# A convolution and whitening kernel: three image groups last instead of two, three x tiles instead of four, and homes for three quarters of the last output piece

## The chip, the core and the metric

The kernel runs on one core of a Trainium2 chip. The metric is the device time of one execution in microseconds (us), and lower is better. The engines are named as the profile names them: PE (matrix products), PEld (its weight loads), DVE (vector), ACT (scalar), POOL and SP. SP issues most DMAs here. A DMA issued by SP or ACT goes through a hardware queue, one issued by POOL through a software queue. All of them move their bytes through the same 16 DMA engines.

## The reference, cut to what matters

Two layers on `x` of shape (4, 64, 256, 256), float32. The first is a long convolution in two dimensions, separable per channel, with filters made by a small sine network. The second whitens the 64 channels: it forms a covariance from every ninth pixel of all four images, takes its inverse square root by five Newton-Schulz steps, and multiplies every pixel by it.

```python
k = jnp.einsum('ijk,imk->ijmk', hx, hy)[0]        # one 256x256 filter per channel
y = jnp.fft.irfft2(u_f * k_f, s=(fft_size, fft_size))[..., :L, :L]
out = y + x * bias[:, None, None]                 # layer 0
...
x1_s = x1[:, ::STRIDE ** 2]
cov = x1_s @ x1_s.T / x1_s.shape[1] + EPS * jnp.eye(B, dtype=x.dtype)
deconv = _isqrt_newton_schulz(cov, N_ITER)
out = deconv @ (x1 - mean1)                       # layer 1
```

No pixel of the output can be made before all four images have gone through layer 0, because the inverse square root needs them all. In what follows "the root" is the short chain from the covariance to the whitening matrix `W`.

## The kernel before, in words

**Convolution.** The 64 channels are cut into 8 groups `g` of 8 channels. A step is one (g, image n) pair, 32 steps in all, and one `x` tile (128 partitions x 4096 float32, 2 MB) holds a step. Inside a step the loop goes over `c` = 0, 2, 4, 6, two channels at a time. I number these quarters of steps by `k = 4 * i + c // 2`, from 0 to 127, and call each one a turn. In turn `k`, `group` (line 394) multiplies the two new channels by the first Toeplitz factor and the two channels of two turns ago by the second one. DVE then adds the bias term in place in the `x` tile (line 412), and `store` (line 420) writes the two finished channels to the DRAM scratch `y_d` with two DMAs of 256 KB.

**Order of the steps.** `steps` (line 107) runs groups 0 to 5 over all images first, and then, image by image, groups 6 and 7. Image 0 is thus complete after step 25, image 1 after 27, image 2 after 29, image 3 after 31. `covariance(n - 1)` (line 572) runs when group 7 of the next image begins, at c = 2, that is in front of the products of turns 109, 117 and 125, and once more after the loop. `blocks` (line 370) says in which turn each of the eight parts of a Toeplitz tile is loaded; three such tiles exist.

**Loads of x.** There are four `x` tiles. In turn (i, c) SP issues the load of the same quarter of step i + 2 (line 588).

**Pieces.** The output is made in 32 pieces of 2 MB (`pieces`, line 344): eight per image, each 128 partitions x 4096. Before the root, pieces can be loaded back from `y_d` into buffers that have become free. There are 13 such homes (line 347): two extra buffers `e`, four sample buffers `s`, three Toeplitz buffers `t`, four x tiles `i`. The table `early` (line 378) gives the turns after which the first nine loads are issued: 106, 108, 110, 112, 117, 120, 124, 125, 126. The other four follow after the last covariance input (line 613). The first piece of image 0 needs `y_d[0]` complete.

**After the root.** For each piece (line 619) PE makes four windows of 1024 columns, ACT and DVE add the shift in place (lines 639 and 640), and the result is stored. Piece 0 goes out in four 512 KB parts, pieces 1, 30 and 31 in two 1 MB parts, all others in one 2 MB store. Stores of pieces 1 to 18 are issued by POOL, the others by SP. After piece i is stored, SP waits for that store and loads piece i + 13 into its home (line 647).

**Queues.** The convolution and the root are written out by hand in each engine's order (`tc.manual_schedule`, line 557). SP carries out its DMAs in that order; a wait at the head of its queue holds back all that follows. Each hardware-queue DMA also takes one of eight semaphores in turn and waits for the DMA that had it before, so at most eight of them are on their way at once.

Of the kernel before, what the change touches and what calls it, by code (L numbers as in the profile page):

```python
# [38 lines left out]
F32 = mybir.dt.float32  # L39
I32 = mybir.dt.int32  # L40
AF = mybir.ActivationFunctionType
ALU = mybir.AluOpType
# [3 lines left out]
NB, C, L = 4, 64, 256  # L46
P, H2 = 128, 2
EMB, ORDER = 33, 64
PIX = L * L
CG = 8  # L50
HP = P // 2
STEP = 9
# [2 lines left out]
EPS = 0.01  # L55
N_ITER = 5
GW = P + L
FP = 4096

TURN = 6.283185  # L60
# [4 lines left out]
def conv_whiten_kernel(ctx: ExitStack, tc: tile.TileContext, a: dict, out: bass.AP):  # L65
# [1 line left out]
    x = a["x"]  # L67

    const = ctx.enter_context(tc.tile_pool(name="const", bufs=1))
    xpool = ctx.enter_context(tc.tile_pool(name="xpool", bufs=4))  # L70
    epool = ctx.enter_context(tc.tile_pool(name="epool", bufs=2))
    spool = ctx.enter_context(tc.tile_pool(name="spool", bufs=NB))
    tpool = ctx.enter_context(tc.tile_pool(name="tpool", bufs=3))
    o1pool = ctx.enter_context(tc.tile_pool(name="o1pool", bufs=4))
# [25 lines left out]
    def load_x(t, g, n, c):  # L100
        nc.sync.dma_start(
            out=t[:, c : c + 2],
            in_=x[n, g][:, c : c + 2],
        )


    steps = [(g, n) for g in range(C // CG - 2) for n in range(NB)]
    steps += [(g, n) for n in range(NB) for g in range(C // CG - 2, C // CG)]

    x_tiles = [xpool.tile([P, CG, H2, L], F32, tag="in", name=f"x{u}") for u in range(4)]  # L110
    for c in range(0, CG, 2):
        load_x(x_tiles[0], *steps[0], c)
        if c == 0:
            nc.sync.dma_start(out=decay, in_=a["decay"])
    nc.sync.dma_start(out=mask, in_=a["mask"])
# [1 line left out]

    ident = const.tile([P, P], F32, tag="ident", name="ident")
    make_identity(nc, ident)
    samp = []  # L120
    for n in range(NB):
        t = spool.tile([P, FP], F32, tag="samp", name=f"samp{n}")
        samp.append(
            t[:, 0 : H2 * NJ * (C + 1)].rearrange("p (b j c) -> p b j c", b=H2, j=NJ)
        )
        nc.gpsimd.memset(samp[n][:, :, :, C : C + 1], 1.0)
        nc.gpsimd.memset(samp[n][:, :, NJ - 1, 0:C], 0.0)
# [199 lines left out]
    def covariance(n):  # L327
# [17 lines left out]


    homes = [
        {"t": (tpool, "toep"), "s": (spool, "samp"), "i": (xpool, "in"), "e": (epool, "extra")}[k]
        for k in "eetssiistitis"
    ]  # L350

    def load_y(i):

        n, q = pieces[i]
        pool, tag = homes[i % len(homes)]
        t = pool.tile([P, FP], F32, tag=tag, name=f"yi_{n}_{q}")
        nc.sync.dma_start(out=t, in_=y_d[n][:, q * FP : (q + 1) * FP])  # L357
        return t

    def load_next():  # L360
        loaded[len(loaded)] = load_y(len(loaded))

    loaded = {}
    todo = []
    pending = []

# [2 lines left out]


    blocks = {}
    for g in range(1, C // CG):
        first = 16 * g - 14 if g < C // CG - 1 else 16 * g - 22
        for part in range(8):
            k = first + (part * 12 // 8 if g < C // CG - 2 else part)
            blocks[k // 4, k % 4 * 2] = (g, part)

    early = {
        (26, 4): 1, (27, 0): 1, (27, 4): 1, (28, 0): 1, (29, 2): 1, (30, 0): 1, (31, 0): 1, (31, 2): 1, (31, 4): 1
    }  # L380
    orders = [list(range(L // HP)), list(reversed(range(L // HP)))]

    credit = [0.0]
# [35 lines left out]

    def store(second):  # L420
        g, n, c, yt, _ = second
        halves = g >= C // CG - 2
        for b in range(H2):
            row = b * C + g * CG + c
            nc.sync.dma_start(
                out=y_d[n][row : row + 2, :].rearrange("c (p w) -> p c w", w=L),
                in_=yt[:, c : c + 2, b],
            )

        if c == CG - 2 and (g, n) != steps[-1]:  # L430
            todo.extend(pack_ops(g, n, yt, slice(CG // 2 if halves else 0, CG)))
        elif c == CG // 2 - 2 and halves:
            todo.extend(pack_ops(g, n, yt, slice(0, CG // 2)))
# [13 lines left out]
    def place(width, rows=P):  # L447
        if not room or room[-1][1] + width > H2 * L:
            t = o1pool.tile([P, H2 * L], F32, tag="o1", name=f"chain{len(room)}")
            room.append([t, 0])  # L450
        t, at = room[-1]
        room[-1][1] += width
        return t[0:rows, at : at + width]
# [6 lines left out]
    def whitening(i15, ones):  # L460
# [86 lines left out]
        Z = Zs[(N_ITER - 2) % 2]  # L547
        pw = product(T, Z, "pw")
        spin(2)
        W = place(C)  # L550
        nc.vector.tensor_scalar(W, pw[:, 0:C], rs, None, ALU.mult)
        shift = const.tile([P, 1], F32, tag="shift", name="shift")
        nc.scalar.activation(shift, pw[:, C : C + 1], AF.Copy, scale=nrs)
# [3 lines left out]
    with tc.manual_schedule(  # L557
        engines={engines.PE, engines.SP, engines.DVE, engines.Activation, engines.Pool}
    ):
        toep = {0: new_toeplitz(0)}  # L560

        for f, lo, hi in ((0, 0, 2), (0, 2, 4), (0, 4, 6), (1, 0, 2), (0, 6, 8), (1, 2, 4), (1, 4, 8)):
            for half in range(2):
                load_toeplitz(toep[0], 0, f, half, lo, hi, nc.scalar if half else nc.sync)
        for c in range(0, CG, 2):
            load_x(x_tiles[1], *steps[1], c)
        for i, (g, n) in enumerate(steps):
            xt = x_tiles[i % 4]
            for c in range(0, CG, 2):
                item = (g, n, c, xt, [])  # L570
                if g == C // CG - 1 and n > 0 and c == 2:
                    covariance(n - 1)
                if len(pending) == 2:
                    group(item, pending.pop(0))
                else:
                    half_group(item, 0)
                pending.append(item)
                if i == 0 and c == 6:

                    fold = const.tile([P, C], F32, tag="fold", name="fold")  # L580
                    nc.vector.tensor_tensor(fold, ident[:, 0:C], ident[:, C:P], ALU.add)

                    nc.scalar.activation(bf[:, 0:1], samp[0][:, 0, 0, C : C + 1], AF.Sqrt)
                if i == 1 and c < CG - 2:
                    load_pick(c // 2 * 3, c // 2 * 3 + 3)

                if i + 2 < len(steps):
                    load_x(x_tiles[(i + 2) % 4], *steps[i + 2], c)
                if (i, c) in blocks:
                    tg, part = blocks[i, c]  # L590
                    if part == 0:
                        toep[tg] = new_toeplitz(tg)
                    lo = part % 2 * CG // 2
                    load_toeplitz(toep[tg], tg, part // 4, part // 2 % 2, lo, lo + CG // 2)
                for _ in range(early.get((i, c), 0)):
                    load_next()
        g, n, c, yt, _ = pending[0]
        for item in pending:
            half_group(item, 1)
            pack(1.0)  # L600
            store(item)

        pack()
        i15 = place(2 * C, rows=C).rearrange("p (u c) -> p u c", u=2)
        for u in range(2):
            nc.gpsimd.tensor_scalar(i15[:, u], ident[0:C, 0:C], 1.5, None, ALU.mult)  # L606
        ones = place(P, rows=C)
        nc.gpsimd.memset(ones, 1.0)
        for lo in range(CG // 2, CG, 2):
            pack_by_pe(g, n, yt, slice(lo, lo + 2))  # L610
        spin(4)
        covariance(NB - 1)
        while len(loaded) < len(homes):
            load_next()
        W, shift = whitening(i15, ones)


    halves = [slice(u * C, (u + 1) * C) for u in range(2)]
    for i, (n, q) in enumerate(pieces):
        yt = loaded.pop(i)  # L620

        v = yt.rearrange("p (v f) -> p v f", v=2)
        o = out[n, q].rearrange("p (v f) -> p v f", v=2)

        part = 512 if i == 0 else 1024 if i == 1 or i > len(pieces) - 3 else 2048
        for w in range(FP // 1024):


            cols = slice(w * 512, (w + 1) * 512)
            po = [  # L630
                psA.tile([P, 512], F32, tag="psA", name=f"po_{n}_{q}_{w}_{u}") for u in range(2)
            ]
            for k in range(2):
                for u in range(2):
                    nc.tensor.matmul(  # L635
                        po[u][halves[k]], lhsT=W[halves[u]], rhs=v[halves[u], k, cols],
                        start=True, stop=True,
                    )
            nc.scalar.activation(v[:, 0, cols], po[0], AF.Identity, bias=shift)  # L639
            nc.vector.tensor_scalar(v[:, 1, cols], po[1], shift, None, ALU.add)  # L640
            end = (w + 1) * 512
            if end % part == 0:

                issue = nc.sync if i == 0 or i + len(homes) >= len(pieces) else nc.gpsimd
                issue.dma_start(out=o[:, :, end - part : end], in_=v[:, :, end - part : end])  # L645
        if i + len(homes) < len(pieces):
            loaded[i + len(homes)] = load_y(i + len(homes))


def _constants():  # L650
# [55 lines left out]
```

## Time and profile before

| what | value |
|---|---|
| median of 3 runs | 902.47 us (902.0 to 902.86) |
| span of the profiled execution | 902.1 us |
| PE busy | 781.2 us, 87% of the span |
| DVE busy | 581.5 us, 64% |
| ACT busy | 395.5 us, 44% |
| moved by DMA | 285.61 MB, 317 GB/s over the span |
| line 220, convolution products, share of the chain that ended last | 64% |
| last convolution product ends | 613.6 us |
| first whitening product begins | 643.25 us |

The profiled execution lasted 902.1 us by its span, which lies inside the range of the three runs and 0.37 us under their median. The profile shows no time around that span. Up to 613.6 us the chain that ended last is almost all PE. From there to 643.25 us it is the packing of the last samples, the last covariance and the root. After that PE is on the chain only for short stretches, and the rest is DMA.

### The profile page before, as it was taken

The numbers are of one execution on the slowest core, as the hardware profiler recorded it, in microseconds if no ns is written. First come the engines' busy times: TensorE is split into PE (matmuls) and PEld (weight loads), VectorE is DVE, ScalarE is ACT, GpSimd is POOL, SyncE is SP. The second block draws the span as 40 slices with busy tenths as digits, with TensorE's granted clock in tenths as the row PEclk, the third lists the DMA queues.
The fourth block names the chain that finished last, engine by engine and source line by source line (L and its number), as shares of the span: only waits on it lengthen the run. The fifth ranks groups of instructions, "written<-read, shape, count | busy, mean of one in ns | idle before, by whom it ended". The sixth has DMA issues, their size and how long they took to land.

```text
span 902.1 us, 28046 instructions
## 1 busy us (share of the span) xinstructions
PE 781.2 (87%) x11928; PEld 647.5 (72%) x11928; DVE 581.5 (64%) x801; ACT 395.5 (44%) x676; POOL 14.5 (2%) x40
## 2 busy tenths in 40 slices
PE   8999999999999999999999999999999565666200
PEld 7999999999999999999999999999533111212000
DVE  3487778877888778877888877877688332233200
ACT  2655554545455555545454444442487232233200
POOL 1000000000000000000000000000010000000000
PEclk9999999999999999999999999999999766866755
DMA  7988889798788888888997899979999999999998
GB/s 209 327 262 252 242 261 271 234 273 251 247 263 261 244 264 259 258 250 267 293 275 241 285 351 356 335 237 390 375 401 429 430 432 432 429 434 430 430 430 355
DMA packets 117912, 285.61 MB, mean 317 GB/s; under 512 B 8891, under 2 KB 91116, under 8 KB 110108
## 3 DMA queue, kind: packets, MB, share of 16 engines
q1 hardware_dynamic: 113436, 244.94, 79.0%
q0 software_dynamic: 3056, 37.95, 10.0%
q8 instruction: 95, 1.56, 0.7%
q10 hardware_dynamic: 1296, 0.93, 0.4%
q14 instruction: 29, 0.24, 0.1%
HBM read 149.35 MB, written 134.44 MB: 315 GB/s over the span
## 4 chain that ended last, share of the span: by engine, by line
PE 74%; DMA 11%; another core or an unknown queue 7%; DVE 0%; issue 0%; SPq 0%; ACT 0%; POOLq 0%; DVEq 0%
PE p L220 64%; DMA out_dram<-yi 5%; DMA yi<-y_d 5%; PE po L635 4%; PE pc L333 2%; PE ph L252 1%; PE pk L300 1%; PE spin L442 1%; DMA toep<-g_d 0%; PE busy L152 0%; PE pm L158 0%; SPq L357 0%; DMA scratch<-in_zw_dram 0%; DVE yi L640 0%
## 5 line engine op out<-in xcount | busy, mean ns | idle before, releaser
L220 PE MATMUL p<-toep,x 64*64 64x64 f32 (+3 forms) x5040 | 579.5, 284 | 0.8 <-issue 0.8
L220 PE MATMUL p<-toep,o 64*64 64x64 f32 (+3 forms) x5040 | 579.5, 284 | 0.0
L220 PEld LDWEIGHTS p<-toep,x 64*128 64x128 f32 (+1 forms) x5040 | 535.7, 166 | 24.4 <-issue 1.3
L220 PEld LDWEIGHTS p<-toep,o 64*128 64x128 f32 (+1 forms) x5040 | 536.7, 166 | 10.7 <-issue 0.2
L409 ACT COPY o<-p 64x512 f32<-64x512 f32 x504 | 292.8, 581 | 294.2 <-PE p L220 286.6
L319 DVE COPY_PREDICATED samp<-mask,x 128x464 f32<-128x464 int32 (+3 forms) x351 | 297.2, 847 | 9.8 <-DVE x L412 0.2
L412 DVE SCALAR_TENSOR_TENSOR x<-x,bias,p 128x512 f32<-128x512 f32 x252 | 179.8, 744 | 121.3 <-PE p L220 117.3
L635 PE MATMUL po<-yi,chain 64*64 64x512 f32 x1024 | 143.7, 720 | 60.4 <-DMA yi<-y_d 60.4
L640 DVE TENSOR_SCALAR yi<-po,shift 128x512 f32<-128x512 f32 x128 | 96.1, 751 | 109.0 <-PE po L635 100.7
L635 PEld LDWEIGHTS po<-yi,chain 64*64 64x64 f32 x1024 | 48.0, 162 | 155.2 <-issue 150.5
L639 ACT ACTIVATE yi<-po,shift 128x512 f32<-128x512 f32 x128 | 88.0, 687 | 116.7 <-PE po L635 116.0
L333 PE MATMUL pc<-samp 128*64 128x65 f32 x464 | 14.9, 223 | 0.0
L333 PEld LDWEIGHTS pc<-samp 128*64 128x64 f32 x464 | 14.3, 137 | 0.3
L645 POOL DMA_DIRECT2D out_dram<-yi x19 | 10.5, 554 | 130.5 <-DMA out_dram<-yi 55.1
L606 POOL TENSOR_SCALAR chain<-ident 64x64 f32<-64x64 f32 x2 | 1.0, 519 | 606.6 <-PE ph L252 606.6
L286 DVE COPY o<-ph 64x256 f32<-64x256 f32 x8 | 3.4, 422 | 9.7 <-PE ph L252 9.6
L152 PE MATMUL busy<-idle 128*128 128x128 f32 x64 | 9.4, 307 | 0.0
L152 PEld LDWEIGHTS busy<-idle 128*128 128x128 f32 x64 | 8.9, 222 | 0.2 <-issue 0.2
L300 PE MATMUL pk<-x,pick 128*128 128x56 f32 (+1 forms) x72 | 8.3, 292 | 0.0
L300 PEld LDWEIGHTS pk<-x,pick 128*128 128x128 f32 x72 | 8.1, 192 | 0.1
L442 PE MATMUL spin<-ident 128*128 128x128 f32 x50 | 7.9, 292 | 0.0
L286 ACT COPY o<-ph 64x256 f32<-64x256 f32 x8 | 2.9, 368 | 10.7 <-DMA toep<-g_d 9.2
(93 smaller groups left out, 77.4 us busy)
## 6 DMA issues: line engine op xcount, KB each, us to landing
x<-in_x_dram SPq DMA_DIRECT2D x128, 512.0 KB, 5.3
y_d<-x SPq DMA_DIRECT2D x256, 256.0 KB, 3.5
yi<-y_d SPq DMA_DIRECT2D x32, 2048.0 KB, 15.6
out_dram<-yi POOLq DMA_DIRECT2D x17, 2048.0 KB, 67.7
out_dram<-yi SPq DMA_DIRECT2D x11, 2048.0 KB, 32.9
toep<-g_d SPq DMA_DIRECT2D x28, 256.0 KB, 6.3
toep<-g_d SPq DMA_DIRECT2D x29, 192.0 KB, 5.7
out_dram<-yi SPq DMA_DIRECT2D x4, 1024.0 KB, 32.8
```

Of the source, the lines that this page charges most:

```text
L152: nc.tensor.matmul(p, lhsT=idle[:, 0:P], rhs=idle[:, P : 2 * P], start=True, stop=True)
L220: mm = nc.tensor.matmul(ps[q : q + w, m, HP * k : L], lhsT=src[parts, k // 2, m * P + q : m * P + q + w], rhs=t[parts, : stop : -1] if k e ...
L300: nc.tensor.matmul(pk[:, b, :, 0:nj], lhsT=pick[:, (s - b) % STEP, :], rhs=yt[:, cs, b, s : s + STEP * (nj - 1) + 1 : STEP], start=(s == 0 ...
L319: nc.vector.copy_predicated(dst, m, src)
L333: nc.tensor.matmul(pc[half], lhsT=samp[n][:, b, j, 0:C], rhs=samp[n][:, b, j, :], start=(b == 0 and j < 2), stop=(b == H2 - 1 and j >= NJ ...
L409: nc.scalar.copy(o1[to], units[u][0][0][fr])
L412: nc.vector.scalar_tensor_tensor(x2[:, c2 + u], x2[:, c2 + u], bias[:, ch : ch + 1], units[u][1][0], ALU.mult, ALU.add,)
L442: nc.tensor.matmul(p, lhsT=ident, rhs=ident, start=True, stop=True)
L635: nc.tensor.matmul(po[u][halves[k]], lhsT=W[halves[u]], rhs=v[halves[u], k, cols], start=True, stop=True,)
L639: nc.scalar.activation(v[:, 0, cols], po[0], AF.Identity, bias=shift)
L640: nc.vector.tensor_scalar(v[:, 1, cols], po[1], shift, None, ALU.add)
L645: issue.dma_start(out=o[:, :, end - part : end], in_=v[:, :, end - part : end])
```

## The change

Six edits go together.

1. `LATE = 3`: groups 0 to 4 run over all images first, then groups 5, 6 and 7 image by image. Image 0 is complete after step 22, image 1 after 25, image 2 after 28, image 3 after 31. The covariances of images 0, 1 and 2 stand in front of turns 97, 109 and 121.
2. Three x tiles instead of four, and three extra buffers instead of two. The x load issued in turn (i, c) is that of step i + 1.
3. A new table for the turns in which Toeplitz tiles are loaded; the last one, for group 7, comes in turns 82 to 86.
4. Early loads are cut into halves of 1 MB: pieces 0 to 3 after turns 98 to 105, piece 4 after 110 and 111, then 5a at 121, 5b and 6a at 122, 6b at 123, 7a, 7b, 8a at 124 to 126, 8b and 9a at 127. 10a, 9b and 10b go between the two last half groups, piece 11 and 12 after the last covariance input. There are again 13 homes, in another order, and the kernel keeps their views instead of taking new tiles from the pools.
5. Three quarters of piece 31 get homes of their own: 512 KB in the selection matrices (`pick`), which are free after the last packing, and four 256 KB tiles of the pool of intermediates (`o1pool`), one of them before and three after the root in SP's order. `W` moves from that pool to a tile of its own.
6. After the root the columns of a window are 1024 consecutive ones, so that a part of a store is one run per partition; the host undoes the layout. Piece 0 goes out in four 512 KB parts, pieces 1 and 30 in two 1 MB parts, piece 31 as six 256 KB stores from the spare homes before piece 30's and one 512 KB store at the end. Stores of pieces 1 to 18 are issued by ACT instead of POOL.

```diff
-    xpool = ctx.enter_context(tc.tile_pool(name="xpool", bufs=4))
-    epool = ctx.enter_context(tc.tile_pool(name="epool", bufs=2))
+    xpool = ctx.enter_context(tc.tile_pool(name="xpool", bufs=3))
+    epool = ctx.enter_context(tc.tile_pool(name="epool", bufs=3))
...
-    steps = [(g, n) for g in range(C // CG - 2) for n in range(NB)]
-    steps += [(g, n) for n in range(NB) for g in range(C // CG - 2, C // CG)]
+    steps = [(g, n) for g in range(C // CG - LATE) for n in range(NB)]
+    steps += [(g, n) for n in range(NB) for g in range(C // CG - LATE, C // CG)]
...
+    def x_of(i):
+        return x_tiles[(i + 1) % 3]
...
     homes = [
-        {"t": (tpool, "toep"), "s": (spool, "samp"), "i": (xpool, "in"), "e": (epool, "extra")}[k]
-        for k in "eetssiistitis"
+        ("e", 0), ("e", 1), ("e", 2), ("s", 0), ("s", 1), ("s", 2), ("t", 5),
+        ("i", 29), ("t", 6), ("i", 30), ("t", 7), ("i", 31), ("s", 3),
     ]
...
+    def load_spare(w, k, t):
+
+        n, q = pieces[-1]
+        lo = q * FP + w * 1024 + k * 512
+        nc.sync.dma_start(out=t, in_=y_d[n][:, lo : lo + t.shape[1]])
+        for v in range(t.shape[1] // 512):
+            spare[w, k + v] = t[:, v * 512 : (v + 1) * 512]
...
+    for g, (first, groups) in {
+        1: (2, 12), 2: (18, 12), 3: (34, 12), 4: (46, 12), 5: (57, 12), 6: (69, 12), 7: (82, 5)
+    }.items():
...
-    early = {
-        (26, 4): 1, (27, 0): 1, (27, 4): 1, (28, 0): 1, (29, 2): 1, (30, 0): 1, (31, 0): 1, (31, 2): 1, (31, 4): 1
-    }
+    early = {98 + v: [(v // 2, v % 2)] for v in range(8)}
+    early.update({110: [(4, 0)], 111: [(4, 1)]})
+    for k, halves in {
+        121: "5a", 122: "5b 6a", 123: "6b", 124: "7a", 125: "7b", 126: "8a", 127: "8b 9a"
+    }.items():
+        early[k] = [(int(h[:-1]), "ab".index(h[-1])) for h in halves.split()]
...
-                if g == C // CG - 1 and n > 0 and c == 2:
+                if g == C // CG - 2 and n > 0 and c == 2:
                     covariance(n - 1)
...
-                if i + 2 < len(steps):
-                    load_x(x_tiles[(i + 2) % 4], *steps[i + 2], c)
+                if 0 < i < len(steps) - 1:
+                    load_x(x_of(i + 1), *steps[i + 1], c)
...
+        load_spare(1, 0, small("spare_0"))
         for lo in range(CG // 2, CG, 2):
             pack_by_pe(g, n, yt, slice(lo, lo + 2))
         spin(4)
         covariance(NB - 1)
-        while len(loaded) < len(homes):
-            load_next()
+        for u in range(2):
+            load_half(11, u)
+        last = const.tile([P, STEP, P], F32, tag="pick", name="spare_pick")
+        load_spare(0, 0, last.rearrange("p a b -> p (a b)")[:, 0:1024])
+        load_y(12)
         W, shift = whitening(i15, ones)
+        for w, k in ((1, 1), (2, 0), (2, 1)):
+            load_spare(w, k, small(f"spare_{w}{k}"))
...
+    def whiten_spare():
+        n, q = pieces[-1]
+        for w in range(3):
+            whiten(w, [spare[w, k] for k in range(2)])
+            for k in range(2):
+                lo = w * 1024 + k * 512
+                nc.sync.dma_start(out=out[n, q][:, lo : lo + 512], in_=spare[w, k])
...
-                issue = nc.sync if i == 0 or i + len(homes) >= len(pieces) else nc.gpsimd
-                issue.dma_start(out=o[:, :, end - part : end], in_=v[:, :, end - part : end])
-        if i + len(homes) < len(pieces):
-            loaded[i + len(homes)] = load_y(i + len(homes))
+                issue = nc.sync if i == 0 or i + len(homes) >= len(pieces) else nc.scalar
+                issue.dma_start(out=out[n, q][:, end - part : end], in_=yt[:, end - part : end])
+        if i + len(homes) < len(pieces) - 1:
+            load_y(i + len(homes))
+        elif i + len(homes) == len(pieces) - 1:
+            load_y(i + len(homes), slice(3 * 1024, FP))
```

## The prediction

> **What bounds the kernel now.** I read the page first, for the engines over time and the chain that ended last.
>
> ```profile
> DMA  7988889798788888888997899979999999999998
> GB/s 209 327 262 252 242 261 271 234 273 251 247 263 261 244 264 259 258 250 267 293 275 241 285 351 356 335 237 390 375 401 429 430 432 432 429 434 430 430 430 355
> PE 74%; DMA 11%; another core or an unknown queue 7%; DVE 0%; issue 0%; SPq 0%; ACT 0%; POOLq 0%; DVEq 0%
> ```
>
> Each slice is 22.55 us. For two thirds of the span the chain is PE; from slice 30 the DMA engines move 430 GB/s to the last slice but one. So the end is set by transfers. While the DMA engines have work, it moves only if bytes go, if a gap in that work closes, or if work is pushed from an idle time into the busy one. I therefore cut the last 430 us into windows (columns: busy time and count of each engine, granted PE clock, DMA share, GB/s).
>
> ```profile
> 473.70:501.40 27.70, 27.70 (x486) 26.05 (x484) 24.78 (x40) 14.12 (x25) 0.00 (x0) 1.00 0.75 236
> 590.00:600.00 10.00, 10.00 (x235) 9.41 (x234) 8.88 (x16) 4.65 (x8) 0.00 (x0) 1.00 0.39 128
> 605.00:610.00 5.00, 5.00 (x118) 4.70 (x116) 3.79 (x7) 2.14 (x4) 0.00 (x0) 1.00 0.90 298
> 610.00:615.00 5.00, 5.00 (x60) 4.68 (x57) 4.86 (x9) 3.36 (x7) 0.00 (x0) 1.00 0.96 331
> 640.00:645.00 5.00, 5.00 (x44) 3.21 (x47) 1.43 (x6) 1.30 (x4) 0.00 (x0) 1.00 0.95 403
> 645.00:650.00 5.00, 5.00 (x52) 1.79 (x48) 4.43 (x7) 4.02 (x7) 0.00 (x0) 1.00 0.70 260
> 650.00:655.00 5.00, 5.00 (x52) 1.84 (x48) 4.36 (x7) 3.97 (x7) 1.42 (x2) 1.00 1.00 375
> 670.00:880.00 210.00, 116.84 (x780) 38.36 (x768) 73.61 (x99) 67.37 (x98) 6.41 (x12) 0.74 1.01 431
> ```
>
> From 600 us on the DMA engines have work nearly all the time; the gaps are at 590 to 600 and at 645 to 650, where the 13 homes are full and the first stores only begin. The third view is SP's own order.
>
> ```profile
> 578.87 0.87 SPq L425 DMA_DIRECT2D y_d<-x  x2
> 579.79 1.32 SPq L357 DMA_DIRECT2D yi<-y_d  x1
> 583.32 15.92 SPq L425 DMA_DIRECT2D y_d<-x  x8
> 599.35 0.40 SPq L357 DMA_DIRECT2D yi<-y_d  x1
> 605.29 1.77 SPq L425 DMA_DIRECT2D y_d<-x  x2
> 607.16 0.41 SPq L357 DMA_DIRECT2D yi<-y_d  x1
> ```
>
> The stores of turns 120, 121 to 124 and 125 are seen here, and the sixth, seventh and eighth piece (579.79, 599.35, 607.16). By 590 us six pieces are in, and no x load is left: the last one went out in turn 119.
>
> **Prices.** A 2 MB piece is 2.097 MB at 431 GB/s: 4.87 us. A turn's two y_d stores: share 0.39 at 590 to 600, one pair in 4.6 us, so 1.8 us of DMA time. Stores and x load of a turn: 0.75 of 27.7 us over six turns, 3.46 us, so the x load is about 1.5 us (floor 0.524 MB at 431 GB/s, 1.22; top 1.67). An x load lands 5.3 us after its issue by the page, of which 3.3 are stores and load, so about 2 us are start and completion.
>
> **The change part by part, on the DMA clock from 582 us on.** Up to turn 120 both kernels are paced by PE, which makes the same products. Covariances 0, 1, 2 (3.64 us each in the chain) come at turns 97, 109, 121 instead of 109, 117, 125, so turns 117 to 120 and 125 to 127 stand where they stood and only turns 97 to 108, 109 to 116 and 121 to 124 are later, by 3.64 us.
>
> *Gaps of before, closed.* 0.61 of 10 us at 590, 0.10 and 0.04 of 5 us at 605 and 610, 0.05 and 0.30 of 5 us at 640 and 645: 6.1 + 0.7 + 1.75 = 8.6 us. After has halves queued at every turn from 121, so I take all of it: −8.6 (bounds −9 and −6).
>
> *A gap opened.* After has five homes up to turn 111; the sixth, the third sample buffer, comes free with covariance 2, which now stands in front of turn 121. From the end of turn 120's transfers (578.9 + 2 + 3.3 = 584.2) to the start of 5a (stores of turn 121 at 583.32 + 3.64 = 587.0, plus 2) the engines are idle: +5 us (4 to 6). Before had the load of 579.79 there.
>
> *x loads pushed into the busy time.* The last step's four quarters went out in turns 116 to 119 and now go in 120 to 123: 4 x 1.5 = +6 us (4.9 to 6.7). I count all four, the first of them ahead of the new gap.
>
> *The spare homes.* 0.75 of a piece is loaded around the root instead of behind it. It is the same work in a busy stretch, so 0; what it could gain is the closing of the gap at 645, counted above. SP's first spare load must wait for the last y_d stores to land, with 10b (2.4 us) as cover: +0.7 (0 to 2).
>
> *Forms of the transfers.* At 650 to 670 piece 0's and 1's parts run at 372 to 397 GB/s, some 2 us lost on 430. After makes their runs twice as long, and adds four loads and six stores of 256 KB. I take −0.7 (−2 to +1.5).
>
> Sum: −8.6 + 5 + 6 + 0.7 − 0.7 = **+2.4 us**; ends −6.1 and +11.2. Since the idle terms exclude each other's extremes I round to +2.2. The span 902.1 stands 0.37 us under the median, so 902.47 + 2.2 = **904.7**.
>
> A cross-check from the other side: behind 589 us after has nine pairs of y_d stores (16.2), three x loads (4.5), pieces 5 to 12 (39.0), three quarters (3.7) and 0.7: 64 us, so its queue runs dry at 653 if no output store joined. The first store comes some 2.3 us after the root, as before at 645.57. So about 7 us of queue reach across the root, and the root itself may be some us later at no cost.
>
> *Costed at nothing.* The new Toeplitz turns: eight parts in turns 82 to 86 behind a share of 0.75 to 0.8; without that cover the first product of turn 88 would wait, some us. Stores from ACT: behind a full DMA queue; each waits for DVE's last add and for the store four earlier, and behind it stand the next piece's evictions, which need 3.5 us per piece (27.7 us for 8 pieces in the chain) against 9.75 us that a store and a load take; without that cover each of 18 stores would cost its handover. POOL is left with nothing there, and no one waits for it.
>
> *A rule that speaks against it.* The Trainium skill, "DMA: Bandwidth & Descriptors", section "Anatomy of one DMA", fits a DMA as 2.0 us fixed plus bytes over 436 GB/s, and its rules for authors ask for 1 MiB or more. The row: the window 540 to 560 has 256 KB stores, 512 KB loads and pieces in one queue at 397 GB/s, so the fixed part overlaps. With sixteen more DMAs in the busy stretch the rule laid end to end would add 32 us, the row nothing; I go by the row.
>
> **The rivals.**
>
> *Faster: the queue is empty at the root.* Then all 13.75 homes are full when W is ready, and 1.57 MB at 430 GB/s, 3.7 us, leave the stage behind it: 898.8. For: the gap at 645 and the idle 590 to 600 are there to be used. Against: the 64 us above. It decides if that work takes under 58 us. Chance 0.15.
>
> *x arrives late.* A quarter is now needed three turns after its issue (3 x 4.6 less 1 us, 12.8 us) instead of seven. In turns 98 to 105 each turn asks for 1.8 + 1.5 + 2.4 = 5.7 us of DMA in 4.6 us, so the queue grows by 1.1 us a turn; the quarter issued in turn 104 lands after some 5.3 + 6.5 = 11.8 us. If the share of 1.04 in the window 540 to 560 means that such a mix costs half a us more a turn, it is 15 us and PE waits 2 to 5 us there; turn 121 moves by as much, and the gap with it: 908. The next turn's quarter is covered by the covariance before turn 109. Against: x loads of before land within 10.0 us at worst. Chance 0.18.
>
> *ACT's stores leave gaps.* If a store waits for a landing with nothing behind it in the queue, 18 handovers at 0.5 us give 9 us: 913. Against: three older stores are queued each time. Chance 0.08.
>
> *Nothing changes:* the terms cancel, 902.5. Chance 0.12.
>
> **How the numbers follow.** The forecast has 0.47, its own range 901 to 907.5. About 0.2% (1.8 us) is what a measurement can tell from no change. Slower than 904.3: 0.27 of the forecast's share, and the two slow rivals, 0.53. Same: 0.18 of the forecast's share and the rival of no change, 0.30. Faster: the first rival and 0.02, 0.17. The range goes from 899.5 to 910, which leaves out part of the first rival and the third.
>
> **What the profile after would show.** Right: no dip at 645 to 650 (over 400 GB/s), a dip to about half between 583 and 589, an x load to landing of 11 to 13 us near turn 105, products of line 226 without waits, 430 GB/s to the end. Wrong: a dip around 640 to 650 (first rival), PE waiting for x tiles (second), GB/s under 425 between 670 and 880 (third). I would also be wrong if the homes before turn 121 were filled at another pace than the table says.

## The result, and the profile after

The changed kernel takes 905.78 us (median of 9 runs, 902.75 to 906.92) against 902.47 us before (9 runs, 901.46 to 902.86). The ratio is 1.003, with an interval of 1.0021 to 1.004: the change makes the kernel about 3 us slower. The forecast was 904.7 us and "slower".

One thing has to be known to read the traces. A kernel's time is 1.8 to 2.0 us longer than its span in all traced executions of the kernels after and of the experiments. The traced execution of the changed kernel has a span of 900.9 us and a time of 902.75 us, so it is the fastest of its nine runs. A second trace of the same kernel has a span of 904.1 and a time of 905.86, close to the median. Both are shown.

The page of the changed kernel: the rows of DMA share and GB/s in 40 slices of 22.5 us, then the chain that ended last.

```profile
DMA  7788788788888898899769988699999999999998
GB/s 215 239 260 261 245 266 258 242 261 259 272 272 265 257 278 259 268 265 288 230 195 376 409 275 293 199 369 412 378 404 430 431 431 431 429 430 427 432 431 341
PE 72%; DMA 20%; DVE 0%; ACT 0%; issue 0%; ACTq 0%; SPq 0%
```

PE still carries most of the chain and the last ten slices but the very last still run at 430 GB/s. The early loads of turns 98 to 105 are seen in slices 22 and 23, which move 376 and 409 GB/s where before had 241 and 285.

Windows of the same trace (columns: busy time and count of PE, PEld, DVE, ACT, POOL; granted PE clock; DMA share; GB/s).

```profile
575.00:580.00 5.00, 5.00 (x162) 4.86 (x160) 4.11 (x8) 1.97 (x4) 0.00 (x0) 1.00 0.71 229
580.00:585.00 5.00, 5.00 (x54) 4.65 (x53) 2.55 (x4) 2.32 (x4) 0.00 (x0) 1.00 0.06 24
590.00:595.00 5.00, 5.00 (x55) 4.65 (x53) 4.83 (x9) 2.32 (x4) 0.00 (x0) 1.00 0.98 299
595.00:600.00 5.00, 5.00 (x120) 4.55 (x117) 4.00 (x8) 2.32 (x4) 0.00 (x0) 1.00 0.99 404
645.00:650.00 5.00, 5.00 (x52) 1.80 (x48) 4.36 (x7) 3.10 (x5) 0.00 (x0) 1.00 0.92 282
680.00:880.00 200.00, 131.91 (x774) 49.47 (x774) 72.84 (x97) 65.84 (x103) 0.00 (x0) 0.78 1.01 430
595.00:630.00 35.00, 34.63 (x553) 32.66 (x550) 25.88 (x46) 9.84 (x19) 1.11 (x3) 1.00 1.03 410
```

The idle time of before at 590 to 600 is gone (0.39 there, 0.98 and 0.99 here), and so, by the share, is most of that at 645 (0.70, now 0.92); the rate there is still low, 282 GB/s after 260. A new idle time stands at 580 to 585, with a share of 0.06. From 595 to 630 the queue is full, at 410 GB/s.

SP's own order in the same trace shows where the new idle time comes from.

```profile
585.44 0.40 SPq L374 DMA_DIRECT2D samp<-y_d  x1
...
632.83 0.33 SPq L384 DMA_DIRECT2D spare<-y_d  x1
639.95 1.50 SPq L384 DMA_DIRECT2D spare<-y_d  x3
643.12 5.21 SPq L696 DMA_DIRECT2D out_dram<-extra  x4
...
667.55 1.31 SPq L374 DMA_DIRECT2D extra<-y_d  x3
```

At 585.44 the first half of the sixth piece is issued. It goes into the third sample buffer, which covariance 2 frees in front of turn 121; the five homes before it have long been full. At 632.83 SP gets past the last stores and begins the spare loads. Piece 0 goes out from 643.12. The next loads come only at 667.55, all at once.

### The profile page after: what moved, and what is told of

Same layout as the page of the kernel before. It is cut to its first block, busy times and chain, and to the rows that moved or that the text cites. A ratio compares the mean times of both kernels' runs of the same rounds, so it can differ in the third digit from the quotient of the medians.

```text
span 900.9 us, 28063 instructions
## 1 busy us (share of the span) xinstructions
PE 798.9 (89%) x11928; PEld 658.8 (73%) x11928; DVE 582.8 (65%) x810; ACT 388.9 (43%) x676; POOL 4.0 (0%) x21
## 4 chain that ended last, share of the span: by engine, by line
PE 72%; DMA 20%; DVE 0%; ACT 0%; issue 0%; ACTq 0%; SPq 0%
PE p L226 64%; DMA extra<-y_d 7%; DMA out_dram<-extra 6%; DMA out_dram<-toep 4%; PE po L664 3%; PE pc L339 2%; DMA samp<-y_d 1%; PE ph L258 1%; PE pk L306 1%; DMA toep<-g_d 0%; PE busy L158 0%; PE spin L476 0%; PE pm L164 0%; DMA scratch<-in_zw_dram 0%; ACT toep L668 0%
## 5 line engine op out<-in xcount | busy, mean ns | idle before, releaser
L226 PEld LDWEIGHTS p<-toep,o 64*128 64x128 f32 (+1 forms) x5040 | 535.6, 166 | 11.7 <-issue 0.8
L664 PE MATMUL po<-samp,W 64*64 64x512 f32 x328 | 51.8, 671 | 5.8 <-DVE samp L669 2.1
L664 PE MATMUL po<-extra,W 64*64 64x512 f32 x288 | 42.0, 683 | 11.5 <-DMA extra<-y_d 8.8
L669 DVE TENSOR_SCALAR samp<-po,shift 128x512 f32<-128x512 f32 x41 | 30.8, 751 | 25.6 <-PE po L664 23.1
L664 PEld LDWEIGHTS po<-samp,W 64*64 64x64 f32 x328 | 19.1, 145 | 37.4 <-DVE samp L669 12.8
L664 PE MATMUL po<-x,W 64*64 64x512 f32 x192 | 35.9, 712 | 11.1 <-ACT toep L668 8.3
L669 DVE TENSOR_SCALAR extra<-po,shift 128x512 f32<-128x512 f32 x36 | 27.0, 751 | 27.6 <-PE po L664 25.7
L664 PE MATMUL po<-toep,W 64*64 64x512 f32 x192 | 37.0, 712 | 7.6 <-ACT samp L668 3.8
L668 ACT ACTIVATE samp<-po,shift 128x512 f32<-128x512 f32 x41 | 26.4, 688 | 39.0 <-DMA out_dram<-extra 15.3
L668 ACT ACTIVATE extra<-po,shift 128x512 f32<-128x512 f32 x36 | 23.4, 688 | 41.6 <-PE po L664 25.6
L669 DVE TENSOR_SCALAR x<-po,shift 128x512 f32<-128x512 f32 x24 | 18.0, 751 | 26.3 <-PE po L664 25.3
L669 DVE TENSOR_SCALAR toep<-po,shift 128x512 f32<-128x512 f32 x24 | 18.0, 751 | 23.6 <-PE po L664 22.6
```

The source lines that it names most:

```text
L226: mm = nc.tensor.matmul(ps[q : q + w, m, HP * k : L], lhsT=src[parts, k // 2, m * P + q : m * P + q + w], rhs=t[parts, : stop : -1] if k e ...
L664: nc.tensor.matmul(po[u][halves[k]], lhsT=W[halves[u]], rhs=halves_of[k][halves[u]], start=True, stop=True,)
L668: nc.scalar.activation(halves_of[0], po[0], AF.Identity, bias=shift)
L669: nc.vector.tensor_scalar(halves_of[1], po[1], shift, None, ALU.add)
```

## Experiments

The theory was now my ledger of DMA time from 582 us on: idle time closed and opened, and work pushed into the busy stretch, decide the end. Its rivals were that the handover of the stores to ACT costs the time, that the root is the bound, and that the spare homes do something else than counted. Each run below is compared with the kernel before, run beside it on the same chip. There are three such groups of runs, in which before took 902.89, 902.91 and 903.0 us. Where two kernels of different groups are compared, the ratios to before are the safer numbers.

### The change once more

Edit: none.

> The changed kernel once more, for a second trace: its nine runs lie between 902.75 and 906.92 us, those of before between 901.46 and 902.86, and the trace at hand is of its fastest run. My theory (the DMA engines start the busy stretch late and never idle again): median 905 to 906.5; in a slower run the products end later or the start of the busy stretch at turn 121 comes later, and from 650 to 880 us the rate is 429 to 432 GB/s. Rival, x arrives late: PE waits for x tiles near turns 104 to 109, 2 to 5 us. Rival, ACT's stores leave gaps: products end as in the first trace, and the rate between 645 and 880 us falls under 425 somewhere.

Measured: 906.51 us (903.27 to 907.74, 6 runs), ratio 1.0036, interval 1.0022 to 1.0049. The slowdown holds. My theory that the DMA engines never idle again in the busy stretch does not: the trace, near the median, has something that the fastest one hardly shows. Windows of 2 us, and the long stretch behind them, same columns:

```profile
668.00:670.00 2.00, 0.00 (x0) 0.00 (x0) 0.00 (x0) 0.00 (x0) 0.00 (x0) 0.82 0.50 213
670.00:672.00 2.00, 0.00 (x0) 0.00 (x0) 0.00 (x0) 0.00 (x0) 0.00 (x0) 0.50 0.05 23
672.00:674.00 2.00, 0.85 (x4) 0.30 (x8) 0.00 (x0) 1.59 (x3) 0.00 (x0) 0.50 0.78 131
680.00:880.00 200.00, 131.46 (x774) 52.52 (x774) 72.80 (x97) 66.14 (x103) 0.00 (x0) 0.79 1.01 429
```

From 668 to 674 the DMA engines are idle for 1.00 + 1.90 + 0.44 = 3.3 us. Nothing like it follows: 429 GB/s from 680 to 880. So it is one hole, not a loss at each store. The chain that ended last goes through it (start, us, what).

```profile
634.73 15.60 DMA samp<-y_d
650.41 21.50 DMA out_dram<-extra
672.01 0.35 ACTq L696
```

And the waits of SP and ACT from 640 to 690 (us in total, times, longest):

```profile
SPq L374 <- DMA out_dram<-extra: 21.1, 3, 11.6
SPq L696 <- DMA samp<-y_d: 4.6, 1, 4.6
```

```profile
ACT samp L668 <- DMA out_dram<-extra: 11.7, 1, 11.7
```

Read from the top: SP issues the four parts of piece 0. The fourth takes a semaphore that the load of piece 12 (`samp<-y_d`) still has, so it waits 4.6 us and goes out at 650.41. It is 512 KB, but stores from ACT are by then on their way beside it, and it lands 21.5 us later. SP's next loads refill piece 0's home and must wait for it; that is a need of the data. ACT waits 11.7 us for the same DMA, and that is not: its store of piece 4 has drawn the semaphore that this part holds, because hardware-queue DMAs of SP and ACT take the same eight in turn. The trace's records name them: the load of piece 12, this fourth part and ACT's store at 672.01 all carry semaphore 100, and the wait that ACT ends at 671.93 is for number 100. While both queues wait for one landing, the rest of the queued transfers run out. In the first trace the fourth part went out at 648.0 and landed at 667.5, and little is lost at 670 to 675 (share 0.94). By the rates in windows of 2 us from 664 to 678, the first trace moves 1.36 MB more than the second, 3.2 us at 430 GB/s. Their spans, 900.9 and 904.1, differ by as much.

### Stores 1 to 18 from POOL again

```diff
-                issue = nc.sync if i == 0 or i + len(homes) >= len(pieces) else nc.scalar
+                issue = nc.sync if i == 0 or i + len(homes) >= len(pieces) else nc.gpsimd
```

> The changed kernel with the stores of pieces 1 to 18 issued by POOL again. My theory: the same as the changed kernel within 1 us, and the same spread over its runs. Rival, ACT's stores leave gaps or share the hardware queue badly with the loads: 3 us faster than the changed kernel and a spread like that of before, under 1.5 us.

Measured: 902.13 us (900.7 to 903.22, 11 runs), ratio 0.999 (0.9982 to 0.9999). The whole slowdown, 906.51 − 902.13 = 4.4 us, comes with the issuing engine, which was the rival; my theory had no difference over 1 us. Windows of this run, and the fourth part of piece 0 (its store at 644.6):

```profile
580.00:585.00 5.00, 5.00 (x54) 4.64 (x54) 2.63 (x4) 2.32 (x4) 0.00 (x0) 1.00 0.11 41
...
665.00:670.00 5.00, 5.00 (x52) 1.80 (x48) 4.36 (x7) 3.97 (x7) 1.07 (x2) 1.00 1.00 424
670.00:675.00 5.00, 5.00 (x52) 1.84 (x48) 4.36 (x7) 3.98 (x7) 0.53 (x1) 1.00 1.01 416
...
DMA to landing us min/median/max: 22.2/22.2/22.2
```

The hole is gone, although the fourth part is as late here, 22.2 us after its issue. SP waits for it as before, but POOL's DMAs carry eight semaphores of their own (111 to 118 in the records), and POOL sends the store of piece 4 at 658.81 without a wait for the fourth part. So the late landing alone makes no hole; it takes a second queue that waits for it. The idle time at 580 stays while the slowdown goes, so it was not what made the kernel slower than before. The runs also scatter less: 2.5 us between the fastest and the slowest, where the unchanged kernel has 4.5.

### Piece 0 from ACT as well

If it is the shared semaphore behind SP's late fourth part, and not ACT as such, then moving piece 0's stores off SP cures it too.

```diff
-                issue = nc.sync if i == 0 or i + len(homes) >= len(pieces) else nc.scalar
+                issue = nc.sync if i + len(homes) >= len(pieces) else nc.scalar
```

> The changed kernel with the four stores of piece 0 issued by ACT too, so that they no longer stand in SP's queue behind the loads. In the second trace of the changed kernel the DMA engines stand still for some 3.5 us around 671, when SP (next load) and ACT (store of piece 4) both wait for the landing of piece 0's fourth part, issued at 650.4 and landed at 671.9. My theory: that one landing is the cost of issuing from ACT; without it the time is that of the kernel with POOL's stores, 902 to 903, the rate between 660 and 680 stays over 400 GB/s, and the spread falls under 2.5 us. Rival, ACT's stores cost at every handover: still 905 to 907.

Measured: 902.57 us (901.75 to 903.72, 11 runs), ratio 0.9997 (0.9988 to 1.0006). That is 0.4 us above POOL's stores, 0.6 by the ratios, and the intervals overlap.

```profile
665.00:670.00 5.00, 5.00 (x49) 2.10 (x41) 4.21 (x6) 3.89 (x6) 0.00 (x0) 1.00 0.99 426
670.00:675.00 5.00, 4.97 (x43) 1.39 (x38) 3.93 (x6) 0.79 (x3) 0.00 (x0) 1.00 1.00 426
```

All stores of pieces 0 to 18 come from ACT here, and there is no hole. So ACT as the issuer costs nothing measurable in itself; what costs is the one part of piece 0 that SP issues late and that then stands in ACT's way. Issued from ACT, ahead of ACT's other stores, the fourth part lands after 10.0 us. That the semaphore is the link rests on the number in the records, on POOL's stores, which pass the same late part on semaphores of their own, and on this run.

### Before, with stores from ACT

```diff
-                issue = nc.sync if i == 0 or i + len(homes) >= len(pieces) else nc.gpsimd
+                issue = nc.sync if i == 0 or i + len(homes) >= len(pieces) else nc.scalar
```

> The kernel before with the stores of pieces 1 to 18 issued by ACT, nothing else. My theory: within 1 us of before. Rival, ACT's stores leave gaps: 2 to 4 us slower, with a spread of some 4 us over the runs.

Measured: 904.25 us (903.21 to 905.77, 11 runs), ratio 1.0016 (1.0007 to 1.0024): 1.4 us, a third of what ACT costs in the changed kernel, and between my theory (within 1 us) and the rival (2 to 4). Its loss lies elsewhere:

```profile
655.00:660.00 5.00, 5.00 (x52) 1.81 (x48) 4.35 (x7) 3.97 (x7) 0.00 (x0) 1.00 1.09 315
820.00:830.00 10.00, 5.16 (x32) 1.74 (x32) 2.00 (x4) 1.83 (x3) 0.00 (x0) 0.66 1.00 410
830.00:840.00 10.00, 6.58 (x60) 2.48 (x60) 5.37 (x8) 4.93 (x8) 0.00 (x0) 1.00 1.01 388
```

The share is 1.0 and the rate is low: engines busy and not idle, at lower GB/s. This is only seen, and its cause is open. The fourth part of piece 0 lands 5.0 us after its issue in this run, so nothing late stands in ACT's way. What follows is that ACT's price belongs to the order of the DMAs around it, and not to ACT alone.

### A longer gap at turn 121

In the kernel with POOL's stores, the loads of turns 121 to 123 go out at turn 124.

```diff
-        121: "5a", 122: "5b 6a", 123: "6b", 124: "7a", 125: "7b", 126: "8a", 127: "8b 9a"
+        124: "5a 5b 6a 6b 7a", 125: "7b", 126: "8a", 127: "8b 9a"
```

> The changed kernel with POOL's stores, and the loads 5a, 5b, 6a, 6b, moved from turns 121 to 123 to turn 124. By the ledger each idle us of the DMA engines at turns 121 to 123 comes back at the end: 1.3 us are left over in each of three to four turns, so 4 to 5 us slower than with POOL's stores alone, 906 to 907. Rival, the queue has slack before the root: 0 to 1 us, 902 to 903.

Measured: 906.42 us (905.65 to 906.67, 5 runs), ratio 1.0039 (1.0025 to 1.0052), 4.3 us above the same kernel without the edit.

```profile
580.00:585.00 5.00, 5.00 (x56) 4.64 (x54) 2.72 (x5) 2.32 (x4) 0.00 (x0) 1.00 0.15 52
585.00:590.00 5.00, 5.00 (x123) 4.81 (x121) 3.80 (x7) 2.32 (x4) 0.00 (x0) 1.00 0.68 216
590.00:595.00 5.00, 5.00 (x54) 4.64 (x54) 4.83 (x9) 2.32 (x4) 0.00 (x0) 1.00 0.83 247
595.00:600.00 5.00, 5.00 (x120) 4.77 (x118) 4.08 (x7) 2.32 (x4) 0.00 (x0) 1.00 0.74 236
```

Without the edit the shares of the last three windows are 1.02, 1.01 and 0.99, so the engines are idle for (0.32 + 0.17 + 0.26) x 5 = 3.75 us more. In GB/s, from 580 to 615, 2.3 MB less are moved, 5.4 us at 430 GB/s. The 4.3 us measured lie between the two. Idle DMA time just ahead of the busy stretch returns at the end, 300 us later, at about its own length. The ledger's way of counting is right here.

### A root that is 3 us later, in both kernels

`spin(14)` puts idle products in front of the last product of the root.

```diff
         Z = Zs[(N_ITER - 2) % 2]
+        spin(14)
         pw = product(T, Z, "pw")
```

In the changed kernel with POOL's stores:

> The changed kernel with POOL's stores and 14 idle products (0.32 us each, 4.5 us less what waits anyway, some 4 us) in front of the last product of the root. My theory: the queue reaches across the root, so 0 to 1.5 us slower, 902 to 903.5. Rival, the root still sets the end: 4 us slower, 906.

In before:

> The kernel before with the same 14 idle products in front of the last product of the root. My theory: its homes are full at the root, so the whole delay shows: 3.5 to 4.5 us slower, 906.5. Rival, the DMA engines have other work there: 0 to 1 us.

Counted from the loads ahead of the root, the first store of piece 0 comes 3.3 us later in the first and 3.0 us later in the second. Measured: 901.76 us (900.46 to 903.35, 11 runs), ratio 0.9988 (0.9979 to 0.9997), against 902.13 without it: nothing. For before, 905.63 us (905.38 to 906.42, 5 runs), ratio 1.0032 (1.002 to 1.0045): +2.7 us, most of the 3.0. Windows of before with the later root, then of the changed kernel with it:

```profile
640.00:645.00 5.00, 5.00 (x45) 4.13 (x48) 0.28 (x1) 0.26 (x1) 0.00 (x0) 1.00 0.47 200
645.00:650.00 5.00, 5.00 (x53) 1.70 (x46) 4.35 (x6) 4.08 (x6) 0.00 (x0) 1.00 0.50 186
```

```profile
640.00:645.00 5.00, 5.00 (x43) 4.21 (x46) 0.28 (x1) 0.26 (x1) 0.00 (x0) 1.00 1.03 419
645.00:650.00 5.00, 5.00 (x52) 1.84 (x48) 4.12 (x6) 3.85 (x6) 0.00 (x0) 1.00 0.99 393
```

With all 13 homes full, before has little to move until the root is done; the changed kernel has its spare homes' and last pieces' loads in the queue and does not notice.

### The spare homes, in before alone and out of the changed kernel

Three quarters of piece 31 get their homes in before, whose schedule stays:

```diff
+        while len(loaded) < len(homes) - 2:
+            load_next()
+        load_spare(1, 0, first)
+        last = const.tile([P, STEP, P], F32, tag="pick", name="spare_pick")
...
         W, shift = whitening(i15, ones)
+        for w, k in ((1, 1), (2, 0), (2, 1)):
+            load_spare(w, k, small(f"spare_{w}{k}"))
```

> The kernel before with homes for three quarters of the last piece (same places as in the change, the first spare load put behind the eleventh piece), nothing else of the change. My theory: the gap of before at 645 to 650 closes, worth 1 to 2 us: 900.5 to 901.5. Rival, each byte loaded ahead of the root is a byte less behind it: 3.7 us faster, 898.8. Rival, nothing: 902.5.

Measured: 900.0 us (898.99 to 902.66, 9 runs), ratio 0.9968 (0.9959 to 0.9978): 2.9 us faster, between my theory and the rival of 3.7. The stretch around the root in this run:

```profile
640.00:645.00 5.00, 5.00 (x47) 2.33 (x50) 2.80 (x5) 2.63 (x5) 0.00 (x0) 1.00 0.97 404
645.00:650.00 5.00, 5.00 (x52) 1.73 (x48) 4.35 (x7) 3.98 (x7) 1.25 (x2) 1.00 1.03 387
```

Before had 0.70 and 260 GB/s at 645 to 650. The three windows behind, 650 to 665, run at 416, 446 and 387 GB/s here and at 375, 369 and 372 in before, so more than the gap is gained; why is not shown. Now the other way round, the changed kernel with POOL's stores and without spare homes:

```diff
-        load_spare(1, 0, small("spare_0"))
...
-        last = const.tile([P, STEP, P], F32, tag="pick", name="spare_pick")
-        load_spare(0, 0, last.rearrange("p a b -> p (a b)")[:, 0:1024])
         load_y(12)
         W, shift = whitening(i15, ones)
-        for w, k in ((1, 1), (2, 0), (2, 1)):
-            load_spare(w, k, small(f"spare_{w}{k}"))
```

> The changed kernel with POOL's stores and without the spare homes: piece 31 is loaded, computed and stored like piece 30. The ledger: the queue before the root is busy either way, so its homes are worth 0 here, 901.5 to 903. Rival, each byte loaded ahead of the root is a byte less behind it: 3.7 us slower than with them, 905.5.

Measured: 901.58 us (899.62 to 902.48, 11 runs), ratio 0.9981 (0.9972 to 0.999). Against the 0.999 of the kernel with the homes that is no loss; if anything it is 0.8 us faster, and the intervals overlap. The share at 640 to 645 falls to 0.75 and 320 GB/s, 1.3 us of idle time, and the end does not show it. So the same homes are worth 2.9 us in one kernel and nothing in the other, and the ledger, by which 1.3 us of idle time return, does not hold here. Why is not settled by these runs; fewer, larger transfers at both ends (one 2 MB load for piece 31 instead of six) may give back as much.

### Consecutive columns alone

Before with windows of 1024 consecutive columns, so that a part of a store is one run per partition:

```diff
-        v = yt.rearrange("p (v f) -> p v f", v=2)
-        o = out[n, q].rearrange("p (v f) -> p v f", v=2)
+        v = yt.rearrange("p (w v f) -> p w v f", v=2, f=512)
...
-                issue.dma_start(out=o[:, :, end - part : end], in_=v[:, :, end - part : end])
+                issue.dma_start(out=out[n, q][:, end - part : end], in_=yt[:, end - part : end])
```

> The kernel before with the columns of a window consecutive, so that each run of the stores of pieces 0, 1, 30 and 31 is twice as long; nothing else. The prediction priced all forms at 0.7 us: 902.2 to 903. If the slow stretch from 650 to 670 us comes from short runs, up to 2 us faster, 901.

Measured: 901.66 us (901.05 to 903.52, 11 runs), ratio 0.999 (0.9981 to 0.9999): 1.3 us by the medians, 0.9 by the ratio. It ran in the same group as the kernel without spare homes (901.58). Those two have the same stores, no spare homes and POOL as issuer, and differ in the schedule: three late groups, three x tiles, halves. The schedule alone is thus worth −0.1 us by the medians and −0.8 by the ratios, which is not told from nothing.

### A version that beats both

If the schedule brings nothing and costs nothing, while spare homes and consecutive columns each gain in before, then before's schedule with both edits, POOL's stores and loads in halves should be the best.

```diff
-LATE = 3
+LATE = 2
...
+        106: "0a 0b", 108: "1a 1b", 110: "2a 2b", 112: "3a 3b", 117: "4a 4b",
+        120: "5a 5b", 124: "6a 6b", 125: "7a 7b", 126: "8a 8b"
...
-                issue = nc.sync if i == 0 or i + len(homes) >= len(pieces) else nc.scalar
+                issue = nc.sync if i == 0 or i + len(homes) >= len(pieces) else nc.gpsimd
```

> The schedule of before (four x tiles loaded two steps ahead, two image groups last, POOL's stores) with the spare homes and the new column layout. If spare homes (2.9 us in the kernel before) and layout add up: 899.5 to 900. If they close the same gap: 900 as with the spare homes alone.

Measured: 899.68 us (897.97 to 900.51, 5 runs), ratio 0.9961 (0.9949 to 0.9974). That is 3.3 us faster than before, but it lies too near to the spare homes alone (900.0, ratio 0.9968) to say whether the two gains add up.

The idle time at 590 is still in it, since its seventh home is filled at turn 124. One more edit brings half of it forward:

```diff
-        120: "5a 5b", 124: "6a 6b", 125: "7a 7b", 126: "8a 8b"
+        120: "5a 5b", 122: "6a", 124: "6b 8a", 125: "7a 7b", 126: "8b 9a"
```

> As the last one, and the seventh piece's first half is loaded after turn 122 instead of 124, where the DMA engines of before stand idle for 6 us (590 to 600), the ninth's and tenth's first halves one turn earlier. By the ledger an idle us filled is a us won at the end: 2.4 us for 1 MB, 897 to 898. Rival, the spare homes' queue already reaches across the root and the stores wait for nothing earlier: 0.

Measured: 898.81 us (897.37 to 899.27, 5 runs), ratio 0.9952 (0.9939 to 0.9964). This is the lowest time of all, but its 0.87 us on the kernel without the edit are not clear of the spread of five runs each. The products end at 610.77 in one trace and at 612.49 in the other, so the windows are set 1.7 us apart: first without the edit, then with it.

```profile
585.00:605.00 20.00, 20.00 (x362) 18.97 (x362) 15.44 (x26) 8.30 (x15) 0.00 (x0) 1.00 0.69 242
640.70:660.00 19.30, 19.30 (x181) 6.88 (x184) 15.91 (x22) 14.62 (x22) 2.74 (x5) 1.00 1.02 417
```

```profile
586.72:606.72 20.00, 20.00 (x363) 18.99 (x362) 15.45 (x26) 8.30 (x15) 0.00 (x0) 1.00 0.82 286
642.42:661.72 19.30, 19.30 (x181) 6.88 (x184) 15.91 (x22) 14.62 (x22) 2.74 (x5) 1.00 1.00 378
```

The 1 MB moved up fills 0.13 of 20 us, 2.6 us, about what was expected. But in the first 19.3 us of the whitening products the rate is 378 GB/s and not 417, at a full share: 0.75 MB less, 1.75 us at 430 GB/s. So most of what was gained ahead of the root is lost behind it in these two traces, by a lower rate and not by idle time. The cause of that rate is open.

## Why the prediction was right, and where it was not

The direction and the time hold, 904.7 against 905.78, inside the forecast's own range. But two errors cancelled in it, so that the number came out so near is luck: the schedule's terms were too dear by some 3 us, and the stores from ACT, costed at nothing, took 4.4.

**The gap opened at turn 121** (+5): right in place and nearly in length. 580 to 585 has a share of 0.06 in the first trace and 575 to 580 one of 0.71, together some 6 us of idle time where I had 4 to 6. Its own price was not measured; making it longer by 3.75 us cost 4.3.

**The queue across the root** (the root may be later at no cost, and the first rival falls): right. Three us of delay cost nothing in the changed kernel with POOL's stores and 2.7 in before. The gap at 590 to 600 closed as counted. My sign of over 400 GB/s at 645 to 650 did not come: 282 GB/s in the first trace, 333 in the second, at shares of 0.92 and 0.96.

**Spare homes at 0** in the changed kernel: right in its outcome, by the run without them, but not by its reasoning, since the idle time at 640 that stands open in that run is not paid for. And the price of the gap at 645 in before, 1.75 us, was short: closing it there gained 2.9.

**Forms of the transfers** (−0.7): right in sign and about in size for the longer runs alone, −0.9 to −1.3; the added small DMAs were not run by themselves. The Trainium skill's page "DMA: Bandwidth & Descriptors", section "Anatomy of one DMA", fits a DMA issued from GpSimd as about 2.0 us fixed plus its bytes over 436 GB/s. Nearly all DMAs here are SP's, and laying the fixed part end to end was my own extension of the page. The run that adds spare homes, halves and consecutive columns to before has more and smaller DMAs and is 3.3 us faster (899.68 against 903.0), so the fixed part stays covered in a full queue.

**The schedule's terms** (−8.6 + 5 + 6, together +2.4): mis-sized. The two kernels that differ in the schedule alone differ by −0.1 us (−0.8 by the ratios). One cause can be read, the x loads at +6. SP issues those of the last step so, in the kernel with POOL's stores:

```profile
576.96 0.44 SPq L102 DMA_DIRECT2D x<-in_x_dram  x1
584.80 0.44 SPq L102 DMA_DIRECT2D x<-in_x_dram  x1
589.74 0.59 SPq L102 DMA_DIRECT2D x<-in_x_dram  x1
594.42 0.84 SPq L102 DMA_DIRECT2D x<-in_x_dram  x1
```

The first goes out ahead of the new idle time and pushes nothing into the busy stretch, yet I counted it. And 1.5 us came from windows that were not full: in the full queue of 595 to 630, at 410 GB/s, an x load of 0.524 MB takes 1.28 us. Three of these are +3.8 and not +6, some 2 of the 3 us. The rest is not split by these runs. From the end of the products on, in before and then with POOL's stores:

```profile
613.60:902.10 288.50, 172.08 (x1357) 73.96 (x1354) 113.66 (x180) 92.20 (x145) 11.68 (x22) 0.77 0.99 416
610.45:899.30 288.85, 170.70 (x1356) 74.06 (x1354) 113.62 (x180) 92.20 (x145) 11.33 (x22) 0.79 0.99 418
```

Rate times length gives 120.0 MB and 120.7 MB still to be moved: 0.7 MB, 1.7 us at 430 GB/s. My terms up to there (+5 + 6, less the gaps of 6.1 and 0.7) say +4.2, so in these two traces the mis-sizing lies ahead of that point.

**Stores from ACT, costed at nothing**: this step failed. It cost 4.4 us. I named as cover a full queue behind each wait and the evictions' slack of 9.75 − 3.5 us; but at the start of the stage one wait is 11.7 us long, on a landing that SP's loads wait for as well, and the cover runs out. I wrote that a store waits for the store four earlier; in fact it waits for whatever DMA, SP's too, last had its semaphore. The third rival had ACT's stores and gaps, as 18 handovers at 0.5 us; there are no 18 gaps (429 GB/s from 680 to 880), there is one hole. The same page's section "Issuing engines are not separate DMA queues" says that DMAs of all issuing engines run on the same 16 DMA engines and interleave, and that the choice saves only issue time. The rates agree from 680 to 880 us, 427 to 430 GB/s with either issuer; the time does not, since what DMAs must wait for also depends on who issues them.

**x arriving late**, the second rival: it fell, and my 11 to 13 us for a landing with it. The loads of turns 98 to 109 in the trace near the median:

```profile
DMA to landing us min/median/max: 4.3/8.2/10.1
```

The products of line 226 show 0.4 us of idle time in the whole run. The queue did not grow by 1.1 us a turn as I worked out; with the smaller price above it would have grown less.

**The base.** I set the profiled span 0.37 us under the median, but a span and a time are not the same. If 1.8 us are added as in the other traces, that execution took about 903.9 us (an estimate), 1.5 above the median. Its products end at 613.6, the latest of the seven traces with before's order of products (610.8 to 613.6).

**Two sums.** The bounds of my terms add up to −2.1 and +10.2, not to −6.1 and +11.2, and 904.7 and 9 us are 913.7. Neither moves the forecast.

## What to carry to other kernels

Before stores are moved to another issuing engine, ask which completion semaphores its DMAs share and with whom: one late landing can stall two queues at once, and the price depends on which DMA holds the semaphore, not on the engine. Idle DMA time ahead of the last busy stretch came back at the end nearly one for one in two tests (a longer gap at turn 121, a later root in before) and did not in two others (no spare homes, a gap filled at 590), while a chain that ends inside a full queue was 3 us later for free. So count it, and then test it with a deliberate delay. Price transfers for a busy stretch by rows of a full queue, and test the edits of a change one by one: here the homes (2.9 us) and the layout (about 1 us) each gained in the old schedule, and the issuing engine (4.4 us) hid both.

## What the runs showed of the hardware that was not expected

- A store of 512 KB, 1.2 us of work at 430 GB/s, took 21.5 us from issue to landing while stores of 1 and 2 MB from ACT were on their way beside it, and 22.2 us beside POOL's. Issued from ACT's own queue it took 10.0 us, and in before with ACT's stores 5.0.
- In these programs the DMAs of SP and ACT carry the same eight semaphores, and those of POOL eight others. A late landing stopped ACT's stores for 11.7 us and POOL's not at all.
- The hole varies from run to run: the DMA engines lose 3.3 us at 668 to 674 in one trace of the unchanged kernel and little in the other, and its times spread over 4.5 us in six runs. Four kernels with POOL's stores spread over 2.5 to 2.9 us in 11 runs each, but before with spare homes, also with POOL's, over 3.7 in nine, so the spread alone does not tell.
- The products of the convolution in before's order, the same instructions, end up to 2.8 us earlier or later in different executions (610.8 to 613.6, seven traces), at a granted clock of 1.00 in all windows shown around it. Some 1 us of this is there when they begin (21.6 to 22.6).
